# Self-attention over four images in split-operand products: the next image's projection moved into the steps of the present image's attention

## The chip, the cores and the metric

The kernel runs on one core of a Trainium2 chip. The core has a matrix engine (PE, with its weight loads shown apart as PEld), a vector engine (DVE), a scalar engine (ACT), a general engine (POOL) and a queue processor (SP). Each executes its own instructions strictly in the order in which the program wrote them and waits for the others by semaphores. POOL and SP issue the transfers between the on-chip memory (SBUF) and device memory (HBM). The metric is the device time of one execution in microseconds.

## The reference, cut to what matters

There are four images of 64 x 64 positions with 256 channels. Each is projected to q and k (128 channels each) and v (256 channels). The arrays are then reshaped, without a transposition, so that attention runs over 4096 columns; the softmax is over the 4096 columns of k.

```python
q = einsum('bwhc,cd->bwhd', x, Wq) + bq      # k with Wk, bk; v with Wv, bv
pq, pk, pv = (t.reshape(B, -1, N) for t in (q, k, v))   # N = 4096
attention = softmax(einsum('bcn,bcm->bnm', pq, pk), axis=-1)
out = einsum('bcm,bnm->bcn', pv, attention).reshape(x.shape)
return gamma * out + x
```

## The kernel before

**Split operands.** The matrix engine is used with operands of type fp32r, one pass for a product instead of fp32's two. To keep the precision, each fp32 operand y is written as three forms: h, a rounded and scaled upper part, l, what is left of y, and d, the slightly enlarged h less y. Three fp32r products of like forms (h by h, l by l, d by d) then stand for the one fp32 product. Each set of forms costs one ACT instruction (h) and two DVE instructions (l and d).

**Projection of an image.** 16 iterations i, each over 256 positions. `transposed` (L115) loads x through SP's queue, makes four PE transposes and one ACT copy. `qk` (L131) makes four fp32 products for q and k, and DVE adds the bias. `v` (L152) does the same for v, with the bias added by ACT. In `project_qk` (L254) ACT and DVE make the forms of q and k, and POOL writes them to HBM in three transfers: `kf` in one of contiguous runs of 3072 bytes a partition, `qd` in two of 1536 bytes. In `halve_v` (L275) the forms of v go to the resident tiles `vh`, `vl`, `vd`. All these products are fp32, two passes each.

**Attention of an image.** 128 steps u: 8 groups of 512 columns of q (index g) by 16 steps t, each with two blocks of 128 columns of k. In step u the code writes, in this order: `cross` for step u+3 (two products d by d, L308, each then scaled in place in PSUM by ACT, L309), the first half of `attend` for u (six products, L365), `energy` for u+2 (four products onto the same banks, L323, and two exponentials on ACT, L326), `upper` for u+2 (the form h of the exponentials, ACT, L332), `load_k` for u+5 (POOL, L296), `halves` for u+1 (DVE: running sum L341, form l L346, form d L348), and the second half of `attend` (six products). So PE has 18 products of 512 columns in a step.

**At a group's end.** `emptied` (L379) reads the four output banks a0, b0, a1, b1 with ACT, `sum_forms` and `sums` add the exponentials over the partitions (two products L396), and the generator `finish` is continued by one piece a step: reciprocal by way of HBM, normalisation on DVE (L410, L418), an accumulating load of x (POOL, L422) and the store (SP, L425).

**Buffers.** The eight PSUM banks are four for energies (`ps_e`) and four for outputs (`ps_o`); the projection borrows from both. Four buffers hold k tiles (`kpool`), three the exponentials x, two the forms `ld`, which the forms of q and k use too. POOL issues a k load as soon as the buffer is free and all POOL instructions written before it are issued.

**Order of images.** Image 0 is projected, then attended; then the projection of image 1 runs (only its first loads and transposes start in the last steps before), and so on. During a projection there is next to no attention work.

Of the kernel before, what the change touches and what calls it, by code (L numbers as in the profile page):

```python
# [9 lines left out]
F32 = mybir.dt.float32  # L10
# [10 lines left out]
def kernel(  # L21
# [54 lines left out]
    xv, ov = columns(x, XB), columns(out, XB)  # L76

    const = ctx.enter_context(tc.tile_pool(name="const", bufs=1))

    def load_x(pool, b, g):  # L80
        t = pool.tile([P, 2, XB], F32, tag="x", name=f"x_{b}_{g}")
        nc.sync.dma_start(t, xv[b, g])
        return t
# [6 lines left out]
    wqk_sb = const.tile([P, KC, 2 * C2], F32, name="wqk_sb")  # L90
    bqk_sb = const.tile([P, 2 * C2], F32, name="bqk_sb")
    nc.gpsimd.dma_start(bqk_sb[:, :C2], bq.partition_broadcast(P))
    nc.gpsimd.dma_start(bqk_sb[:, C2:], bk.partition_broadcast(P))
    wv_sb = const.tile([P, KC, C], F32, name="wv_sb")
    nc.gpsimd.dma_start(wv_sb, wv.rearrange("(k p) e -> p k e", p=P))
    bv_sb = const.tile([P, KC], F32, name="bv_sb")
    for eh in range(KC):
        nc.gpsimd.dma_start(bv_sb[:, eh : eh + 1], bv[eh * P : (eh + 1) * P].unsqueeze(1))
    gam2 = const.tile([P, 2], F32, name="gam")
    gam, gam1 = gam2[:, :1], gam2[:, 1:]  # L100
    nc.gpsimd.dma_start(gam, gamma.partition_broadcast(P))

    class Projection:


        def __init__(self, b, xpool, psum, xt_out, qk_out, v_out):
            self.b, self.xpool, self.psum = b, xpool, psum
            self.xt_out, self.qk_out, self.v_out = xt_out, qk_out, v_out
            self.xs, self.xt = {}, {}

        def load(self, g):
            if g < NI and g not in self.xs:
                self.xs[g] = load_x(self.xpool, self.b, g)

        def transposed(self, i):  # L115

            for g in range(i, i + 2):
                self.load(g)
            pool, tag = self.psum()
            tp = pool.tile([P, KC, 2, P], F32, tag=tag, name=f"xt_{self.b}_{i}")  # L120
            for k in range(KC):
                for s in range(2):
                    nc.tensor.transpose(
                        tp[:, k, s, :],
                        self.xs[i][:, s, k * P : (k + 1) * P],
                        ident,
                    )
            self.xt[i] = self.xt_out(i)
            nc.scalar.copy(self.xt[i], tp)  # L129

        def qk(self, i):  # L131
            pool, tag = self.psum()
            qk = pool.tile([P, 2, 2 * C2], F32, tag=tag, name=f"qk_{self.b}_{i}")
            for s in range(2):
                for k in range(KC):
                    nc.tensor.matmul(  # L136
                        qk[:, s, :],
                        self.xt[i][:, k, s, :],
                        wqk_sb[:, k, :],
                        start=(k == 0),  # L140
                        stop=(k == KC - 1),
                    )
            for dst, o in self.qk_out(i):
                w = dst.shape[2]
                nc.vector.tensor_tensor(  # L145
                    dst,
                    qk[:, :, o : o + w],
                    bqk_sb[:, o : o + w].unsqueeze(1).to_broadcast([P, 2, w]),
                    ALU.add,
                )  # L150

        def v(self, i):  # L152
            pool, tag = self.psum()
            vp = pool.tile([P, KC, C], F32, tag=tag, name=f"v_{self.b}_{i}")
            for eh in range(KC):
                for k in range(KC):
                    nc.tensor.matmul(  # L157
                        vp[:, eh, :],
                        wv_sb[:, k, eh * P : (eh + 1) * P],
                        self.xt[i][:, k].rearrange("p s a -> p (s a)"),  # L160
                        start=(k == 0),
                        stop=(k == KC - 1),
                    )
            to, bias, scale = self.v_out(i)
            for eh in range(KC):
                nc.scalar.activation(  # L166
                    to[:, eh, :],
                    vp[:, eh, :],
                    AF.Identity,
                    bias=bias[:, eh : eh + 1],  # L170
                    scale=scale,
                )
# [7 lines left out]
    E = 2.0**-12  # L180


    UPPER = 1.0 - 2.0**-13

    xg, og = columns(x, NB), columns(out, NB)
    again = const.tile([P, 1], I32, name="again")
    zs = const.tile([P, 1], F32, name="zs")
    rall = const.tile([P, B * NG, NJ], F32, name="rall")
    bv4_sb = const.tile([P, KC], F32, name="bv4_sb")
    nc.gpsimd.tensor_scalar(bv4_sb, bv_sb, 1.0 / E, None, ALU.mult)  # L190
    nc.gpsimd.tensor_scalar(gam1, gam, 1.0 + E, None, ALU.mult)

# [6 lines left out]
    with ExitStack() as fast:  # L199
# [4 lines left out]
        xpool, xtpool, qkv = pool("xpool", 3), pool("xtpool", 3), pool("qkv", 1)  # L204
        ppool = pool("ppool", 2)
        work = pool("work", 2)
        kpool = pool("kpool", 4)
        dram = pool("dram", 2, space=DRAM)
        ps_e = pool("ps_e", 4, space=PSUM)
# [3 lines left out]
        vh, vl, vd = (  # L213
            qkv.tile([P, NM, C], F32R, tag=name, name=name) for name in ("vh", "vl", "vd")
        )
        zd, rd = (dram.tile([B * NG, NB], F32, tag=n, name=n, bufs=1) for n in ("zd", "rd"))
        nc.scalar.dma_start(wqk_sb[:, :, :C2], wq.rearrange("(k p) d -> p k d", p=P))
        nc.scalar.dma_start(wqk_sb[:, :, C2:], wk.rearrange("(k p) d -> p k d", p=P))

        images, qd, kf, units, loads, now = [], {}, {}, {}, {}, {}  # L220

        energies = cycle([(ps_e, "e")])
        outputs = cycle([(ps_o, "a0"), (ps_o, "a1"), (ps_o, "b0"), (ps_o, "b1")])
        active = []

        def start(pieces):
            active.append(pieces)
            next(pieces)
# [5 lines left out]

        def image(b):
            def xt_out(i):
                return xtpool.tile([P, KC, 2, P], F32, tag="xt", name=f"xts_{b}_{i}")

            def qk_out(i):
                now["qk"] = work.tile([P, 2, 2, C2], F32, tag="qk", name=f"qks_{b}_{i}")  # L240
                return tuple((now["qk"][:, w], w * C2) for w in range(2))

            def v_out(i):
                now["v4"] = work.tile([P, KC, C], F32, tag="v4", name=f"v4_{b}_{i}")
                return now["v4"], bv4_sb, 1.0 / E

            images.append(Projection(b, xpool, lambda: next(now["banks"]), xt_out, qk_out, v_out))

            for g in range(NG):
                qd[b, g] = dram.tile([P, NJ, 3, P], F32R, tag=f"qd{g}", name=f"qd_{b}_{g}")  # L250
            for t in range(NU):
                kf[b, t] = dram.tile([P, 2, 3, P], F32R, tag=f"kf{t}", name=f"kf_{b}_{t}")

        def project_qk(b, i):  # L254
            images[b].qk(i)
            qk = now["qk"]
# [8 lines left out]
            for s in range(2):  # L265
                nc.gpsimd.dma_start(qd[b, i // NJ + NG // 2 * s][:, i % NJ], f[:, 0, s])
# [430 lines left out]
```

## Time and profile before

The three runs shown took 2433.49, 2436.36 (median) and 2436.83 us.

| what | value |
|---|---|
| time of the profiled execution | 2433.35 us |
| its span | 2431.6 us, granted PE clock 0.997 |
| busy share PE / PEld / DVE / ACT / POOL | 98% / 81% / 85% / 76% / 18% |
| 512-column fp32r products (18 x 512 steps) | 9216 |
| period of a group of 16 steps | 66.47 us |
| moved through the DMA queues | 338.22 MB, mean 139 GB/s |

PE's busy share counts a product from its issue to its modelled end, and neighbours overlap; so what a product costs is read from the distance between starts, not from its duration. In the groups of instructions the number after x is how many there are, then come total busy time, mean duration, and the idle time before them with what ended it. A line of the timeline has start, length, engine, line of the code, operation and tiles; several like instructions in a row are merged, and then the length runs from the first start to the last end. A group's period is read from any instruction that occurs once a group.

### The profile page before, as it was taken

What the parts mean: (1) busy time and instruction counts of PE and PEld (TensorE: products, weight loads), DVE (VectorE), ACT (ScalarE), POOL (GpSimd) and SP (SyncE); (2) the same over time, 40 slices, a digit from 0 to 9 for tenths busy, and PEclk for the clock granted to TensorE, in tenths of its full rate; (3) what the DMA queues carried; (4) which work ended last, traced back from release to release, by engine and by line L of the source; (5) the groups of instructions that cost most, each with busy time, mean ns of one, the idle gap of its engine ahead of it and who ended that gap; (6) DMA issues with size and microseconds to landing.
All of it is one profiled execution on the core that took longest, in us unless ns stands there. A gap on an engine that the chain in (4) does not pass through costs nothing.

```text
span 2431.6 us, 30522 instructions
## 1 busy us (share of the span) xinstructions
PE 2385.8 (98%) x10588; PEld 1963.4 (81%) x10588; DVE 2071.1 (85%) x2058; ACT 1851.9 (76%) x3071; POOL 429.2 (18%) x781
## 2 busy tenths in 40 slices
PE   9999999999999999999999999999999999999998
PEld 7788888888778888888887888888888788888886
DVE  5888888888698888888879888888887988888887
ACT  5778778777578878778767778787776777878775
POOL 4211111111321111111032111111113111111110
PEclk9999999999999999999999999999999999999999
DMA  8544444454854444444485544444448544444443
GB/s 257 155 123 123 127 120 122 132 133 104 248 164 128 116 129 116 128 130 127 107 263 155 129 130 117 126 118 126 130 105 266 150 128 132 125 118 129 114 124 90
DMA packets 155215, 338.22 MB, mean 139 GB/s; under 512 B 23471, under 2 KB 56751, under 8 KB 155054
## 3 DMA queue, kind: packets, MB, share of 16 engines
q0 software_dynamic: 114656, 293.52, 44.8%
q1 hardware_dynamic: 39854, 42.41, 6.0%
q8 instruction: 87, 1.43, 0.2%
q14 instruction: 74, 0.61, 0.1%
q10 hardware_dynamic: 544, 0.26, 0.0%
HBM read 268.89 MB, written 67.24 MB: 138 GB/s over the span
## 4 chain that ended last, share of the span: by engine, by line
PE 80%; ACT 11%; DMA 4%; DVE 2%; issue 2%; POOL 0%; ACTq 0%; DVEq 0%; POOLq 0%
PE a L365 34%; PE e L323 17%; PE b L365 17%; PE e L308 8%; DMA qd<-f 4%; ACT o L379 3%; ACT h L332 2%; ACT s L326 1%; PE qk L136 1%; ACT x L326 1%; PE z L396 1%; PE v L157 1%; ACT v L166 1%; ACT f L259 1%; ACT e L309 1%
## 5 line engine op out<-in xcount | busy, mean ns | idle before, releaser
L326 ACT ACTIVATE x<-e 128x512 f32<-128x512 f32 x960 | 520.8, 595 | 402.2 <-PE e L323 402.2
L341 DVE TENSOR_TENSOR s<-s,x 128x1024 f32<-128x1024 f32 x480 | 587.4, 1224 | 167.7 <-ACT x L326 159.0
L365 PE MATMUL b<-ld,vd 128*128 128x512 f32 x2048 | 632.1, 390 | 4.3 <-DVE ld L348 4.1
L365 PE MATMUL a<-ld,vl 128*128 128x512 f32 x2048 | 631.1, 389 | 4.8 <-DVE ld L346 4.8
L365 PE MATMUL a<-h,vh 128*128 128x512 f32 x2048 | 631.7, 390 | 0.5 <-ACT v L166 0.5
L346 DVE TENSOR_TENSOR ld<-x,h 128x1024 fp32r<-128x1024 f32 x480 | 584.5, 1218 | 3.7 <-DMA qd<-f 3.7
L348 DVE SCALAR_TENSOR_TENSOR ld<-h,x 128x1024 fp32r<-128x1024 f32 x480 | 584.6, 1218 | 0.0
L296 POOL DMA_DIRECT2D k<-kf x512 | 273.7, 535 | 1680.0 <-PE e L323 1546.9
L323 PE MATMUL e<-q,k 128*128 128x512 f32 x2048 | 548.7, 390 | 0.7 <-ACT e L309 0.7
L309 ACT ACTIVATE e<-e 128x512 f32<-128x512 f32 x1024 | 544.8, 566 | 0.0
L332 ACT ACTIVATE h<-x 128x1024 fp32r<-128x1024 f32 x480 | 509.9, 1062 | 14.9
L365 PEld LDWEIGHTS b<-ld,vd 128*128 128x128 f32 x2048 | 383.2, 188 | 89.0 <-DVE ld L348 7.5
L365 PEld LDWEIGHTS a<-ld,vl 128*128 128x128 f32 x2048 | 384.0, 188 | 86.6 <-DVE ld L346 6.5
L323 PEld LDWEIGHTS e<-q,k 128*128 128x128 f32 x2048 | 383.6, 188 | 81.4 <-ACT e L309 1.6
L365 PEld LDWEIGHTS a<-h,vh 128*128 128x128 f32 x2048 | 384.1, 188 | 80.1 <-ACT v L166 1.0
L308 PE MATMUL e<-q,k 128*128 128x512 f32 x1024 | 318.6, 392 | 0.0
L308 PEld LDWEIGHTS e<-q,k 128*128 128x128 f32 x1024 | 191.9, 188 | 44.5 <-ACT x L326 6.1
L261 DVE SCALAR_TENSOR_TENSOR f<-f,qks 128x512 fp32r<-128x512 f32 x128 | 82.8, 688 | 67.8 <-ACT f L259 67.8
L136 PE MATMUL qk<-wqk_sb,xts 128*128 128x256 f32 x512 | 125.3, 388 | 2.1 <-ACT xts L129 1.9
L157 PE MATMUL v<-xts,wv_sb 128*128 128x256 f32 x512 | 120.8, 380 | 0.0
L259 ACT ACTIVATE f<-qks 128x512 fp32r<-128x512 f32 x64 | 40.4, 631 | 100.9 <-DVE qks L145 58.5
L136 PEld LDWEIGHTS qk<-wqk_sb,xts 128*128 128x128 f32 x512 | 95.0, 193 | 17.7 <-ACT xts L129 5.2
(68 smaller groups left out, 1040.2 us busy)
## 6 DMA issues: line engine op xcount, KB each, us to landing
k<-kf POOLq DMA_DIRECT2D x512, 384.0 KB, 3.4
kf<-f POOLq DMA_DIRECT2D x64, 384.0 KB, 3.1
qd<-f POOLq DMA_DIRECT2D x128, 192.0 KB, 3.8
q<-qd POOLq DMA_DIRECT2D x32, 768.0 KB, 5.1
x<-in_x_dram SPq DMA_DIRECT2D x64, 256.0 KB
o<-in_x_dram POOLq DMA_DIRECT2D x31, 512.0 KB, 5.9
out_dram<-o SPq DMA_DIRECT2D x31, 512.0 KB
r<-rd SPq DMA_DIRECT2D x31, 256.0 KB
```

The lines of the kernel that those rows point to most:

```text
L136: nc.tensor.matmul(qk[:, s, :], self.xt[i][:, k, s, :], wqk_sb[:, k, :], start=(k == 0), stop=(k == KC - 1),)
L157: nc.tensor.matmul(vp[:, eh, :], wv_sb[:, k, eh * P : (eh + 1) * P], self.xt[i][:, k].rearrange("p s a -> p (s a)"), start=(k == 0), stop= ...
L296: nc.gpsimd.dma_start(t, kf[b, u % NU])
L308: nc.tensor.matmul(e, *forms(b, u, i, 2), start=True, stop=False, skip_group_check=True)
L309: nc.scalar.mul(e, e, -1.0 / (1.0 + E))
L323: nc.tensor.matmul(e, *forms(b, u, i, f), start=False, stop=(f == 1), skip_group_check=True)
L326: nc.scalar.activation(x[:, i, :], e, AF.Exp, scale=(1.0 + E) / E)
L332: nc.scalar.activation(h, units[b, u], AF.Identity, scale=UPPER)
L341: nc.vector.tensor_tensor(s, s, x, ALU.add)
L346: nc.vector.tensor_tensor(l, x, h.bitcast(F32), ALU.subtract)
L348: nc.vector.scalar_tensor_tensor(d, h.bitcast(F32), 1.0 + E, x, ALU.mult, ALU.subtract)
L365: nc.tensor.matmul(to, (vh, vl, vd)[f][:, t + NU * i, j * P : (j + 1) * P], units[b, u][f][:, i, :], start=(t == 0 and i == 0 and f != 1), ...
```

## The change

The projection of image b+1 no longer stands between two attentions. It is cut into 16 iterations of eight steps each, and runs inside the 128 steps of image b's attention. The function `step` is called three times in each step, for the PE, the ACT and the DVE part; r is the step's number in its eight.

- The projection's products become fp32r: x gets forms h, l, d (`x_forms`), the weights get theirs once at the start (`weights`, into `wf`), and `products` makes 12 products of 256 columns for q and k and 12 for v in place of four fp32 products each. The d-by-d products come first; `seed_qk` (DVE) and `seed_v` (ACT) scale that partial sum in PSUM and add the bias; the other eight accumulate on top.
- PE: transposes at r = 0, d-by-d products at r = 3 and 5, the others at r = 4 and 6. ACT: one form at r = 1, 5 and 7, two seeds at r = 6. DVE: one instruction of 128 x 512 in each step but r = 4.
- The forms of q and k of an iteration lie in another order, with q and k side by side in each form. POOL writes them at r = 6 in four transfers, each of three runs of 512 bytes a partition.
- The forms of v of images 1 to 3 are written to HBM (`vf`, 6144 bytes a partition) at the next r = 0, and read back into the one resident tile `vall`, one sixteenth a step from three steps after the last group's start (`load_v`, POOL).
- `cross` is now for step n+2, in the same step as its `energy`. `load_k` is for n+4 and stands after the step's POOL writes. The energies have two PSUM banks instead of four, the projection two of its own, k tiles have three buffers instead of four, the exponentials two instead of three. The second `emptied` of a group and `sums` move to the next group's first step. `finish` has its pieces spaced differently.
- Image 0 is projected ahead of its attention, in the same split products; its v forms go straight to `vall`. The attention's steps are numbered through all images.

```diff
--- before.py
+++ after.py
...
-        xpool, xtpool, qkv = pool("xpool", 3), pool("xtpool", 3), pool("qkv", 1)
+        qkv = pool("qkv", 1)
         ppool = pool("ppool", 2)
         work = pool("work", 2)
-        kpool = pool("kpool", 4)
+        kpool = pool("kpool", 3)
         dram = pool("dram", 2, space=DRAM)
-        ps_e = pool("ps_e", 4, space=PSUM)
+        ps_e = pool("ps_e", 2, space=PSUM)
+        ps_p = pool("ps_p", 2, space=PSUM)
         ps_o = pool("ps_o", 1, space=PSUM)
-        vh, vl, vd = (
-            qkv.tile([P, NM, C], F32R, tag=name, name=name) for name in ("vh", "vl", "vd")
-        )
+        vall = qkv.tile([P, NU, 3, 2, C], F32R, tag="v", name="v")
+        wf = qkv.tile([P, 2, 3, KC, C], F32R, tag="wf", name="wf")
...
+        def split(h, l, d, y, scale=E):
+
+            nc.scalar.activation(h, y, AF.Identity, scale=UPPER * scale)
+            yield
+            for t, f in ((l, 1.0 / scale), (d, 1.0 / scale + 1.0)):
+                nc.vector.scalar_tensor_tensor(t, h.bitcast(F32), -f, y, ALU.mult, ALU.add)
+                yield
...
+        def load_x(b, i):
...
+        def x_forms(b, i):
...
+            h = f[:, 0]
+            nc.scalar.activation(h, y, AF.Identity, scale=UPPER)
+            yield
+            nc.vector.tensor_tensor(f[:, 1], y, h.bitcast(F32), ALU.subtract)
+            yield
+            nc.vector.scalar_tensor_tensor(f[:, 2], h.bitcast(F32), 1.0 + E, y, ALU.mult, ALU.subtract)
+            yield
+
+        def products(b, i, w, fs):
+
+            xf = units["xf", b, i]
+            if fs[0] == 2:
+                units[w, b, i] = bank(f"qv{w}_{b}_{i}", [P, 2, C])
+            to = units[w, b, i]
+            for f in fs:
+                for s in range(2):
+                    for k in range(KC):
+                        if w:
+                            left, right = wf[:, 1, f, k, s * P : (s + 1) * P], xf[:, f, k]
+                        else:
+                            left, right = xf[:, f, k, s, :], wf[:, 0, f, k]
+                        nc.tensor.matmul(
+                            to[:, s, :],
+                            left,
+                            right.rearrange("p s a -> p (s a)") if w else right,
+                            start=(f == 2 and s == k == 0),
+                            stop=(f == 1 and k == KC - 1),
+                            skip_group_check=True,
+                        )
+
+        def seed_qk(b, i):
+            y = units[0, b, i]
+            nc.vector.scalar_tensor_tensor(
+                y, y, REST, bias.unsqueeze(1).to_broadcast([P, 2, C]), ALU.mult, ALU.add
+            )
+
+        def seed_v(b, i):
+            y = units[1, b, i]
+            for eh in range(KC):
+                nc.scalar.activation(
+                    y[:, eh, :], y[:, eh, :], AF.Identity, bias=bvs[:, eh : eh + 1], scale=REST
+                )
+
+        def qk_forms(b, i):
+            y = units.pop((0, b, i))
+            f = work.tile([P, 2, 3, C], F32R, tag="pf", name=f"f_{b}_{i}")
+            h = f[:, :, 0, :]
+            nc.scalar.activation(h, y, AF.Identity, scale=UPPER / 64)
+            yield
...
+                nc.vector.scalar_tensor_tensor(f[:, :, j, :], h.bitcast(F32), s, y, ALU.mult, op)
+                yield
-            nc.gpsimd.dma_start(kf[b, i], f[:, 1])
             for s in range(2):
+                nc.gpsimd.dma_start(kf[b, i // 2 + NU // 2 * s][:, i % 2], f[:, s, :, C2:])
+                nc.gpsimd.dma_start(qd[b, i // NJ + NG // 2 * s][:, i % NJ], f[:, s, :, :C2])
...
+        def v_forms(b, i):
+            y = units.pop((1, b, i))
+            units.pop(("xf", b, i))
+            if b == 0:
+                f = vall[:, i]
+            else:
+                f = work.tile([P, 3, 2, C], F32R, tag="pf", name=f"vf_{b}_{i}")
+            yield from split(f[:, 0], f[:, 1], f[:, 2], y)
+            if b:
+                nc.gpsimd.dma_start(vf[b, i], f)
+
+        def load_v(b, t):
+            nc.gpsimd.dma_start(vall[:, t], vf[b, t])
...
+        def load_k(n):
+            b, u = divmod(n, STEPS)
+            if b < B:
                 t = kpool.tile([P, 2, 3, P], F32R, tag="k", name=f"k_{b}_{u}")
                 nc.gpsimd.dma_start(t, kf[b, u % NU])
...
+        def step(n, engine):
+
+            b, u = divmod(n, STEPS)
+            i, r = divmod(u, R)
+            b += 1
+            made = now["made"]
+            if engine == "pe" and b < B:
+                if r == 0:
+                    transposed(b, i)
+                elif r == 3:
+                    products(b, i, 0, (2,))
+                elif r == 4:
+                    products(b, i, 0, (0, 1))
+                elif r == 5:
+                    products(b, i, 1, (2,))
+                elif r == 6:
+                    products(b, i, 1, (0, 1))
+            elif engine == "act" and b < B:
+                if r == 1:
+                    made["x"] = x_forms(b, i)
+                    next(made["x"])
+                    load_x(b, i + 1)
+                elif r == 5:
+                    made["qk"] = qk_forms(b, i)
+                    next(made["qk"])
+                elif r == 6:
+                    seed_v(b, i)
+                elif r == 7:
+                    made["v"] = v_forms(b, i)
+                    next(made["v"])
+            elif engine == "dve":
+                if r == 0 and "v" in made:
+                    for _ in made.pop("v"):
+                        pass
+                if b < B:
+                    if r in (1, 2):
+                        next(made["x"])
+                    elif r == 3:
+                        seed_qk(b, i)
+                    elif r == 5:
+                        next(made["qk"])
+                    elif r == 6:
+                        for _ in made.pop("qk"):
+                            pass
+                    elif r == 7:
+                        next(made["v"])
...
+        for i in range(NI):
+            load_x(0, i + 3)
+            if i + 1 < NI:
+                transposed(0, i + 1)
+                xs = x_forms(0, i + 1)
+            else:
+                xs = iter(())
+            products(0, i, 0, (2,))
+            seed_qk(0, i)
+            products(0, i, 1, (2,))
+            next(xs, None)
+            seed_v(0, i)
+            if i in (12, 14):
+                cross(i // 2 - 6)
+            products(0, i, 0, (0, 1))
+            qk = qk_forms(0, i)
+            next(qk)
+            products(0, i, 1, (0, 1))
+            if i in (12, 14):
+                energy(i // 2 - 6)
+            vs = v_forms(0, i)
+            next(vs)
+            for _ in xs:
+                pass
+            for _ in qk:
+                pass
+            for _ in vs:
+                pass
+            if i in (13, 15):
+                upper(i // 2 - 6)
             if i == 6:
...
+                load_q(0, 0)
+            if i in (6, 7, 8, 13):
+                load_k(i - 6 if i < 13 else 3)
+        halves(0)
+        now["banks"] = cycle([(ps_p, "p")])
+        for n in range(B * STEPS):
+            b, u = divmod(n, STEPS)
+            g, t = divmod(u, NU)
+            final = n == B * STEPS - 1
+            if u == 0 and b + 1 < B:
+                image(b + 1)
+                load_x(b + 1, 0)
+            if n == B * STEPS - 6:
+                xr = ppool.tile([P, 2, NB], F32, tag="s", name="xr")
...
+            cross(n + LOOK)
+            if t == 0 and n:
+                emptied(n - 1, 1)
+            if t == NU - 1 and not final:
+                sum_forms(n)
+            step(n, "act")
+            if not final:
+                attend(n, 0)
+            energy(n + LOOK)
+            if t == 0 and n:
+                sums(n - 1)
+                active.append(finish(n // NU - 1, now["o"], now["total"]))
+            if t == NU - 1 and not final:
+                emptied(n, 0)
+            upper(n + LOOK)
+            step(n, "pe")
+            halves(n + 1)
+            step(n, "dve")
+            if final:
+                finish_last(n, xr)
+                break
+            attend(n, 1)
+            load_k(n + LOOK + 2)
+            if t == 6 and n + NU < B * STEPS:
+                load_q(*divmod(n // NU + 1, NG))
+            if n >= STEPS - NU + 3 and (n - 3) // NU % NG == NG - 1 and (n - 3) // STEPS + 1 < B:
+                load_v((n - 3) // STEPS + 1, (n - 3) % NU)
+            proceed()
```

The helpers not shown (`transposed`, `load_x`, `weights`, `image`, `bank`) hold what the text above says of them, and the class `Projection` is kept for the fallback at the kernel's end, which the runs don't enter.

## The prediction

> **What bounds the kernel now.** I read the page first, for shares and rows:
>
> ```profile
> span 2431.6 us, 30522 instructions
> PE 80%; ACT 11%; DMA 4%; DVE 2%; issue 2%; POOL 0%; ACTq 0%; DVEq 0%; POOLq 0%
> L296 POOL DMA_DIRECT2D k<-kf x512 | 273.7, 535 | 1680.0 <-PE e L323 1546.9
> L261 DVE SCALAR_TENSOR_TENSOR f<-f,qks 128x512 fp32r<-128x512 f32 x128 | 82.8, 688 | 67.8 <-ACT f L259 67.8
> ```
>
> PE carries the chain of waits, and POOL waits 3.4 us for each k load (1546.9 over 450): k is early today. Then busy time by stage: image 0's projection, its attention, image 1's projection.
>
> ```profile
> 7.00:78.00 71.00, 68.56 (x340) 58.34 (x338) 49.25 (x92) 44.54 (x90) 27.46 (x53) 1.00 0.86 259
> 78.00:608.00 530.00, 524.95 (x2305) 430.83 (x2305) 465.42 (x418) 417.10 (x679) 78.33 (x140) 1.00 0.47 123
> 608.00:684.00 76.00, 70.91 (x340) 59.66 (x338) 51.52 (x94) 47.39 (x94) 28.62 (x55) 0.98 0.79 237
> ```
>
> The third column before the end is the PE clock, the last two are DMA share and GB/s: projection is where the DMA engines are busy. Then one step in the timeline, to time the change step by step:
>
> ```profile
> 300.10 0.61 PE L308 MATMUL e<-q,k 128*128 128x512 f32 x2
> 300.57 1.06 ACT L309 ACTIVATE e<-e 128x512 f32<-128x512 f32 x2
> 301.88 1.22 DVE L348 SCALAR_TENSOR_TENSOR ld<-h,x 128x1024 fp32r<-128x1024 f32 x1
> 301.91 1.07 PE L323 MATMUL e<-q,k 128*128 128x512 f32 x4
> 302.56 1.09 ACT L326 ACTIVATE x<-e 128x512 f32<-128x512 f32 x2 [0.93 <-PE e L323]
> 303.28 0.53 POOL L296 DMA_DIRECT2D k<-kf  x1 [3.02 <-PE e L323]
> 303.68 1.06 ACT L332 ACTIVATE h<-x 128x1024 fp32r<-128x1024 f32 x1
> 304.18 0.61 PE L308 MATMUL e<-q,k 128*128 128x512 f32 x2
> ```
>
> A step is 304.18 - 300.10 = 4.08 us, 18 products at 0.2267, PE without a gap. ACT has 0.93 free, DVE 0.58.
>
> **Removed: three projections.** The last `emptied` of images 0, 1, 2 stands at 607.90, 1212.70, 1814.77 in the chain of waits; less eight groups of 66.47 the two distances leave 73.0 and 70.3. With their mean for the third: -214.9.
>
> **Added on PE: 48 iterations of four transposes and 24 products of 256 columns.** No such fp32r product is in the trace. The rows nearest:
>
> ```profile
> 2419.59 0.30 PEld L457 LDWEIGHTS rp<-last,ones 128*128 128x128 f32 x2 [0.86 <-DVE last L445]
> 662.87 0.60 PE L123 MATMUL xt<-ident,x 128*128 128x128 f32 x4
> 663.30 1.89 PE L136 MATMUL qk<-wqk_sb,xts 128*128 128x256 f32 x8
> ```
>
> An instruction alone lasts 276 ns (L123) and 388 (L136), so starts stand (600 - 276)/3 = 108 and (1890 - 388)/7 = 215 ns apart. The 107 ns between them are 128 columns at the two-pass pace, so 256 at the fp32r pace; 512 cost 227. One product of 256 thus costs from 113 (half) to 227 - 107 = 120; I take 117. The weight load is the doubt: it lasts 188 ns, and if it can't hide, a product costs 188 + 4 = 192, the upper end. I take it as hidden, since two loads in a row (first line) last 0.30 together, so follow each other by 0.11. One iteration is 4 x 0.108 + 24 x 0.117 = 3.24; 48 make +155.7.
>
> A rule speaks against this. The Trainium skill, "TensorE: Matmul & The Clock Gate", Part 3 (packing small matmuls), says that a weight load overlaps matmuls in flight only for another row group; every load here takes all rows. By it a product is an estimated 107 + 109 = 216 ns and the sum 114 us more. The trace disagrees: a 188 ns load and 512 columns fit into 227.
>
> **Image 0's projection** is bound by DVE: seven instructions of 0.62 (L261's 0.688, starts 0.6 to 0.65 apart) and a wait of 0.7 for the q and k form, 5.0 an iteration where PE needs 3.24. The narrow writes (below) add 4.05 us of transfer to x's 0.93, 4.98, so a DMA share near 1; I take 5.4. 16 make 86; ahead of them stand the weights' four ACT and four DVE instructions (first product at 10 instead of 8.5), behind them the last forms and two early energies, some 7. Step 1 begins near 104 instead of 83.92: +20. Bounds: +3 (DVE's 4.35 alone) to +37 (POOL at 6.6, below).
>
> **Inside a step** r of the eight, from its first product: cross to 0.45, attend to 1.81, energies to 2.72, projection, attend. ACT scales until 1.5, then its projection instruction (0.6; two of 0.41 at r = 6) fits into the free 0.93 before the exponentials at 2.46: nothing; without that cover 0.6 us in each of four steps of eight. Two energy banks suffice, as the exponentials end at 3.5, before the next cross at 4.08. DVE needs 3.42 + 0.62 = 4.04 against PE's mean of 4.08 + 3.24/8 = 4.49: nothing, though without the gap it would cost up to 0.6 a step. x loads (SP, 7 steps ahead), reads of `vf` (13 steps ahead) and the respaced `finish` hide behind those distances; the reads bring the last group's transfers to some 4.4 us a step, just under its length.
>
> **Group's end.** `emptied` now delays the scaling (PE 0.46) and the products of `sums` wait for its second half (0.7): 1.16 instead of 0.6 seen before L396. +0.56 a group; in image 3's eight groups +4.
>
> **The k load behind four narrow writes** decides. At r = 6 POOL issues the q and k writes, then k for n+4. It can't overtake, and the step's first product two steps on waits for it. DVE ends the last form at 3.2 (l at 0.2, d 1.35, form 2.5); at t = 14 the half-sum (L352, 0.68) makes it 3.85. The write's POOL time is not in the trace with 384 runs: 128 runs take 0.53; the weight load L95 with 256 took 0.736 next to 0.56, the accumulating load L422 with 256 took 1.095. So 0.53 to 1.65, and I take 0.87 from L95, the only plain one. Four take 3.5, and k is issued at 6.7. It lands 3.4 later:
>
> ```profile
> DMA to landing us min/median/max: 3.0/3.4/9.2
> ```
>
> at 10.1. The transfer says later: single packets in the trace took 80 ns for 1536 bytes, 136 for 3072 and 249 for 6144, a line that gives 42 for 512; 1536 of them on 16 engines last 4.05, and k's own 1.09 and its fixed part of 2.3 come behind, 10.7. I take 10.4. Needed it is at 5.02 (r = 6) + 4.08 (r = 7) = 9.1. Late by 1.3 and, at t = 14, by 1.95; the second covers the group's 0.6. Net 2.65 a group, 24 groups: +64. Bounds: +13 (in time, only the 0.56 left) to +198 (POOL 1.65: late 4.1 and 4.75).
>
> At r = 0 the v form's write (0.53 on POOL, 2.0 of transfer at 249 ns for 6144 bytes) goes ahead of k in the same way: DVE ends it at 3.75, k is issued at 4.3 and lands between 7.7 and 9.0; needed at 4.08 + 0.44 + 4.08 = 8.6. I take nothing; at most 0.4 a group, 10 in all.
>
> **Sum.** 2431.6 - 214.9 + 155.7 + 20 + 4 + 64 = 2460.4 span. The profiled execution took 1.75 more than its span and was 3.0 below the median; so in terms of the median I forecast 2465, 1.2% slower.
>
> **Rivals.**
> - *Faster: k is in time.* Place: POOL's queue at r = 6. Price: 64 becomes 13, so 2414. It decides if the four writes and k's landing fit into the 5.9 us between 3.2 and 9.1, that is if k is issued by 5.7. For: POOL's rows are flat at 0.53 from 1536 to 6144 bytes a run; if they are flat in the number of runs too, k is issued at 5.3; and landings go down to 3.0. Against: the transfer of 4.05. The Trainium skill, "DMA: Bandwidth & Descriptors", Anatomy of one DMA, calls descriptor generation small, many descriptors coming before it shows; by that this case holds, but L95 (0.736 to 0.56) leans the other way.
> - *Weight loads bind the 256-column products* (192 ns): +24 x 48 x 0.075 = +86, so 2549. The skill's rule above would put it higher still. For: 188 ns exceed 107. Against: the 0.30 for two loads.
> - *POOL pays by L422's row:* +134 on the k load and +17 ahead, 2614. Against: L422 also accumulates.
>
> **Chances.** Forecast 0.52 (2435 to 2490), k in time 0.33 (2398 to 2430), weight loads 0.09, POOL 0.06. What a measurement of this kernel tells from no change is about 0.2%, 4.9 us. The seam of the first two, 2431 to 2441, holds 0.04. So faster 0.32, same 0.04, slower 0.64. The range reaches from inside the faster case to short of the weight-load one: 2402 to 2535, which leaves out 0.04 below and 0.13 above.
>
> **What would show it.** The distance between starts of the 256-column products (0.117 against 0.192). A PE gap at the first product of steps with r = 0, released by the k load: 1 to 2 us twice a group in images 0 to 2, none in image 3. POOL's duration for `kf` and `qd` writes (0.87 against 0.53 or 1.65). The start of step 1 near 104. A group's period near 75.6 in images 0 to 2 (73.5 if k is in time), 67 in image 3. Wrong I am if the gap is missing, or if DVE or ACT rather than k is what PE waits for within a step.

## The result, and the profile after

The changed kernel took 2588.49 us (median of four runs, 2586.50 to 2592.37), the kernel before beside it 2435.41: a ratio of 1.0631, 95% interval 1.0613 to 1.0649. It is 6.3% slower, 153 us, where 1.2% was forecast and the range ended at 2535. The profiled execution took 2586.5 us.

The page of the changed kernel: span, busy shares, the costliest rows, and the landing times of two queues.

```profile
span 2584.7 us, 31929 instructions
PE 2392.0 (93%) x11096; PEld 1968.0 (76%) x11096; DVE 2150.5 (83%) x2126; ACT 1881.7 (73%) x3075; POOL 582.3 (23%) x942
L286 POOL DMA_DIRECT2D k<-kf x512 | 284.9, 557 | 1153.6 <-PE e L314 934.7
L299 PE MATMUL e<-q,k 128*128 128x512 f32 x1024 | 325.6, 399 | 140.3 <-DMA k<-kf 138.2
L260 POOL DMA_DIRECT2D kf<-f x128 | 98.4, 769 | 518.1 <-ACT x L317 221.1
k<-kf POOLq DMA_DIRECT2D x512, 384.0 KB, 4.1
vf<-vf POOLq DMA_DIRECT2D x48, 768.0 KB, 4.5
```

PE was 98% busy and is now 93%. The row of the cross products (L299) says why: 138.2 us of idle PE end with a k load. The rows of POOL give the price that was unknown: a narrow write is 769 ns, a k load 557. By stage (image 0's projection, then the attention of images 0, 2 and 3; image 1's is like image 2's; the columns as in the table before the change):

```profile
7.00:109.70 102.70, 71.58 (x496) 65.21 (x497) 78.52 (x123) 51.69 (x98) 54.69 (x73) 0.97 0.89 190
109.70:745.00 635.30, 591.38 (x2745) 486.50 (x2743) 529.28 (x522) 466.74 (x761) 144.87 (x233) 0.99 0.59 162
1390.00:2036.00 646.00, 596.35 (x2768) 489.19 (x2768) 537.66 (x530) 471.46 (x768) 149.17 (x240) 0.99 0.62 170
2036.00:2574.00 538.00, 533.04 (x2318) 434.84 (x2319) 464.97 (x421) 418.49 (x679) 80.53 (x143) 1.00 0.49 131
```

In the last stage, where nothing of a next image is left, PE is 99% busy and the DMA share 0.49; an attention before the change had 0.47. In the stages with a projection inside, PE stands idle for 44 to 50 us an image although the DMA engines are busy for only 0.6 of the time. One stretch of image 0's attention shows both places. First POOL (two issues between 377.67 and 384.76, a load of q and the next step's k load, are left out):

```profile
374.58 0.76 POOL L260 DMA_DIRECT2D kf<-f  x1 [9.71 <-ACT x L317]
375.34 0.79 POOL L261 DMA_DIRECT2D qd<-f  x1
376.12 0.78 POOL L260 DMA_DIRECT2D kf<-f  x1
376.89 0.78 POOL L261 DMA_DIRECT2D qd<-f  x1
377.67 0.59 POOL L286 DMA_DIRECT2D k<-kf  x1
384.76 0.54 POOL L272 DMA_DIRECT2D vf<-vf  x1 [5.43 <-issue]
385.29 0.54 POOL L286 DMA_DIRECT2D k<-kf  x1
385.81 1.15 POOL L411 DMA_DIRECT2D o<-in_x_dram  x1
```

and PE's lines of the two products that wait, each behind the last product of the step before:

```profile
379.49 0.61 PE L356 MATMUL b<-ld,v 128*128 128x512 f32 x2
381.91 0.70 PE L299 MATMUL e<-q,k 128*128 128x512 f32 x2 [1.80 <-DMA k<-kf]
390.21 0.61 PE L356 MATMUL b<-ld,v 128*128 128x512 f32 x2
392.42 0.70 PE L299 MATMUL e<-q,k 128*128 128x512 f32 x2 [1.59 <-DMA k<-kf]
```

The first wait (r = 0) is the one that was forecast: four writes at r = 6, k issued behind them at 377.67. The second (r = 2) was costed at nothing: the v form's write at 384.76 goes ahead of the k load at 385.29, and that load is in place only when PE starts at 392.42. So two late k loads stand in each eight steps, four in a group. In images 0 to 2, from the second group on, the mean length of a step (the distance between the cross products of neighbouring steps) is 6.11 us at r = 7 (it holds the wait at the next r = 0), 5.20 at r = 1, and 4.08 for a plain step.

### The profile page after: what moved, and what is told of

Its sections match the earlier page's. It is cut to its first block, busy times and chain, and to the rows that moved or that the text cites. A ratio compares the mean times of both kernels' runs of the same rounds, so it can differ in the third digit from the quotient of the medians.

```text
span 2584.7 us, 31929 instructions
## 1 busy us (share of the span) xinstructions
PE 2392.0 (93%) x11096; PEld 1968.0 (76%) x11096; DVE 2150.5 (83%) x2126; ACT 1881.7 (73%) x3075; POOL 582.3 (23%) x942
## 5 line engine op out<-in xcount | busy, mean ns | idle before, releaser
L356 PE MATMUL a<-h,v 128*128 128x512 f32 x2048 | 643.4, 395 | 0.0
L356 PE MATMUL a<-ld,v 128*128 128x512 f32 x2048 | 639.0, 393 | 2.4 <-DVE ld L337 2.4
L356 PE MATMUL b<-ld,v 128*128 128x512 f32 x2048 | 638.8, 393 | 0.1
L299 PE MATMUL e<-q,k 128*128 128x512 f32 x1024 | 325.6, 399 | 140.3 <-DMA k<-kf 138.2
L356 PEld LDWEIGHTS a<-ld,v 128*128 128x128 f32 x2048 | 387.3, 189 | 87.6 <-DVE ld L337 2.9
L356 PEld LDWEIGHTS b<-ld,v 128*128 128x128 f32 x2048 | 387.9, 190 | 85.1 <-ACT s L386 1.4
L356 PEld LDWEIGHTS a<-h,v 128*128 128x128 f32 x2048 | 370.8, 190 | 63.7 <-issue 0.6
L299 PEld LDWEIGHTS e<-q,k 128*128 128x128 f32 x1024 | 186.0, 189 | 208.5 <-issue 97.3
L228 PE MATMUL qv<-wf,xf 128*128 128x256 f32 x768 | 115.9, 287 | 24.0 <-DVE qv L239 22.5
L228 PEld LDWEIGHTS qv<-wf,xf 128*128 128x128 f32 x768 | 107.4, 191 | 35.5 <-DVE qv L239 25.6
L228 PEld LDWEIGHTS qv<-xf,wf 128*128 128x128 f32 x768 | 107.7, 192 | 7.5
L228 PE MATMUL qv<-xf,wf 128*128 128x256 f32 x768 | 112.8, 283 | 0.0
```

The lines of the kernel that those rows point to most:

```text
L228: nc.tensor.matmul(to[:, s, :], left, right.rearrange("p s a -> p (s a)") if w else right, start=(f == 2 and s == k == 0), stop=(f == 1 an ...
L299: nc.tensor.matmul(e, *forms(n, i, 2), start=True, stop=False, skip_group_check=True)
L356: nc.tensor.matmul(to, vall[:, t, f, i, j * P : (j + 1) * P], units[n][f][:, i, :], start=(t == 0 and i == 0 and f != 1), stop=(t == NU - ...
```

## The experiments

The kernel before took 2433.63, 2434.49 and 2434.59 us (medians) beside the three groups of experiments below.

### Which write makes which wait

Three kernels issue a k load ahead of the step's writes: in every step (`k_first`), only at r = 6, ahead of the q and k writes (`k_first_qk`), only at r = 0, ahead of the v write (`k_first_v`). In all other steps of the last two it keeps its place.

```diff
+            if not final:                   # k_first; k_first_qk: if n % R == 6
+                load_k(n + LOOK + 2)        # k_first_v: if n % R == 0
             step(n, "dve")
...
             attend(n, 1)
-            load_k(n + LOOK + 2)
```

> Edit: in every step the k load for n+4 stands ahead of the step's POOL writes instead of behind them; nothing else. In the changed kernel a group takes 80.3 us in images 0 to 2 where PE's own work is 66.95 + 2 x 3.31 = 73.6. Theory A (order in POOL's queue: k is issued only after the writes): the waits of the cross products for k (138 us, 83 times) vanish, and with them the 18 windows of half PE clock; a group takes 73.6 to 74.5, the kernel 2588 - 24 x 6.3 = 2435, between 2420 and 2450. Theory B (the DMA engines are too full for k in these steps whatever the order): k is issued earlier but still lands late; a group stays above 78, the kernel above 2540.

> Edit: the k load goes ahead of the four narrow q and k writes (r = 6) only; behind the write of the v forms (r = 0) it stays. Theory A: of some 6.7 us a group the two late loads of r = 6 carry 1.8 + 2.2 and most of the half-clock windows, so 2588 - 24 x 4.5 = 2480. As I predicted it (the v write costs at most 0.4 a group) it would be 2440 or less, the whole loss but 10 us. Theory B: above 2560.

> Edit: the k load goes ahead of the v write (r = 0) only; behind the narrow q and k writes it stays. Theory A: 2588 - 24 x 2.2 = 2535, the rest of what the load ahead of all writes gives, so that the two parts add up to it within 15 us. As I predicted it: 2578 or more. Theory B: above 2570.

| k load ahead of | median us | ratio to before (95%) | PE waits for k | step length at r = 7 / 0 / 1 / 2 |
|---|---|---|---|---|
| nothing (the change) | 2588.49 | 1.0631 (1.0613 to 1.0649) | 138.2 us, 83 times | 6.11 / 5.41 / 5.20 / 4.28 |
| the q and k writes | 2584.35 | 1.0617 (1.0596 to 1.0638) | 112.2 us, 55 times | 4.08 / 5.52 / 6.46 / 4.87 |
| the v write | 2536.6 | 1.0421 (1.0393 to 1.0449) | 93.0 us, 52 times | 6.00 / 5.39 / 4.10 / 4.29 |
| both | 2463.45 | 1.0118 (1.0101 to 1.0135) | 25.2 us, 25 times | 4.08 / 5.48 / 4.11 / 4.64 |

Step lengths are means over images 0 to 2 from the second group on.

Each move takes away exactly its own wait, so the order in POOL's queue is the cause of both: r = 7 falls to 4.08 with the first, r = 1 to 4.10 with the second. But the times don't add. Against the kernel with k ahead of both, the q and k writes in front of the load cost 73 us, the v write in front of it costs 121, and both together 125. The two waits stand in for each other. In `k_first_qk` the v write is issued 4.81 us after its step's first product (388.08 against 383.27), in the changed kernel 2.85 after (384.76 against 381.91): the v form doesn't move along with PE's wait, so when the wait at r = 0 goes, the write and the k load behind it stand that much later in the step, and what the step at r = 1 takes above a plain one grows from 1.1 to 2.4. The expectation for `k_first_qk` (2480) missed that; the one for `k_first_v` (2535) was met.

`k_first` stayed 28 us above its expectation. Its waits for k, in the view of waits:

```profile
PE e L299 <- DMA k<-kf: 25.2, 25, 4.0
```

stand for the most part in one place: 17 of the 25, 18 of the 25 us, are at t = 11, for the k load written at t = 9. On POOL it comes behind the v write of t = 8 and behind the accumulating load of x (L411) that follows it, and takes 7.6 us on average to land. The long landing is not the v write's doing: in `k_first_sp` below, where the v write has left POOL's queue and L411 has not, the same load still takes 7.0 us. But there it is issued 1.3 us before its step's first product, here 1.5 after, because POOL stands at the v write until the v form is done.

### Is it the transfers' shape, or the queue?

One kernel lays the forms of q and k out so that each write has one run of 1536 bytes a partition in place of three of 512. One leaves the order of the program as it is and issues the writes from SP's queue. One does that and has k ahead too.

```diff
-            f = work.tile([P, 2, 3, C], F32R, tag="pf", name=f"f_{b}_{i}")      # runs_1536
+            f = work.tile([P, 2, 2, 3, C2], F32R, tag="pf", name=f"f_{b}_{i}")
...
-            nc.gpsimd.dma_start(vf[b, i], f)                                    # sp_writes; kf, qd alike
+            nc.sync.dma_start(vf[b, i].bitcast(F32), f.bitcast(F32))
```

> Edit: the forms of q and k lie so that each of the four writes has one run of 1536 bytes a partition instead of three of 512; order and bytes as in the changed kernel. POOL's time for a write falls from 0.77 to 0.53 us (four: 1.0 less) and their transfer from about 4.0 to 2.4. k is issued 1.0 earlier and lands 1.0 to 2.0 earlier, so the late loads of r = 6 (1.8 and 2.2 us) shrink to about 0.6 and 1.0, and those of r = 0 stay: 2588 - 24 x 2.6 = 2525. If only the order counts and not the size of the runs: above 2570.

> Edit: the writes of the q, k and v forms are issued by SP instead of POOL; the k loads keep their place in the code, so nothing stands before them in POOL's queue but other loads and the accumulating x load. Theory A, order in POOL's queue: as with the k load moved ahead of all writes, 2463, between 2445 and 2480. Rival, shared transfer: the writes still move 192 KB and 768 KB through the same 16 DMA engines beside the k loads and k stays late: above 2540. A third outcome, a gain of about half (2490 to 2530), would say that issue order and transfer each carry a part.

> Edit: k load ahead of the step's writes, and the writes issued by SP. What is left in the k-first kernel is a wait of 0.6 to 1.6 us at t = 10, where the k load issued one step after the v write lands 7.3 us after its issue behind that write (4.3) and the accumulating load (7.1). If POOL's order is behind that too, the writes on SP end it: a group falls from 74.7 to 73.6, the kernel from 2463 to 2435. If it is the transfer, a group stays at 74.5 and more, the kernel at 2458 to 2475.

`runs_1536` took 2619.51 us (1.0762, 1.0740 to 1.0783), slower than the change. POOL's write did fall, from 769 to 536 ns, and the wait at r = 0 with it (5.34 at r = 7 instead of 6.11); but r = 1 went from 5.20 to 6.21 and r = 2 from 4.28 to 4.95, as in `k_first_qk`. PE's waits for k fall from 89.9 to 50.4 us at r = 0 and rise from 44.5 to 92.5 at r = 2, and the time at half the PE clock (below) rises from 61 to 96 us. The expected 2525 missed the second wait again.

`sp_writes` took 2431.79 us (0.9990, 0.9976 to 1.0005), level with the kernel before and better than either case expected. The same bytes in the same pieces move over the same DMA engines, and the waits for k are gone. Two of its lines of waits, and its page's line of the k loads:

```profile
PE e L303 <- DMA k<-kf: 1.0, 2, 0.7
PE xt L197 <- DMA x<-in_x_dram: 7.4, 2, 4.0
```

```profile
k<-kf POOLq DMA_DIRECT2D x512, 384.0 KB, 3.3
```

What has changed is when k is issued. The loads written at r = 6 and r = 0 now go out 0.9 to 1.4 us before the first product of their step (means); in the changed kernel it was 6.9 to 7.6 us after it at r = 6 and 3.5 to 4.5 after it at r = 0. The landing is not free of the writes. Most k loads of `sp_writes` meet none: 152 that met no write and none of POOL's other loads took 3.4 us on average, while the 16 that had at least half of a v form's write beside them took 5.3. Issued so early, they have that time. So what made k late is its place behind the writes in POOL's program, where POOL first stands until the forms are done; the added traffic costs about 2 us of landing where the two meet; and the shape of the writes, by `runs_1536`, is no cure while that place stays. The second line of waits is the same trap on SP: at the start of images 1 and 2 the load of x, which the changed kernel issued more than 25 us ahead, stands behind the last q and k writes, and PE waits for it once each.

With k ahead as well (`k_first_sp`) it is 2426.21 us (0.9975, 0.9959 to 0.9992), below the 2435 that was expected if POOL's order was behind the rest; PE's waits for k are 1.3 us there, where `k_first` had 25.2.

### What the gaps do to PE's clock

The changed kernel's trace has 18 windows of 3.4 us at half the PE clock, 61 us in all besides the end; the kernel before has a granted clock of 0.997, this one 0.986. Sixteen of them begin within 1.5 us of the end of a PE gap of 1.8 to 3.4 us that a k load ended; the other two are in image 0's projection. Not every gap has its window: there are 31 of 1.8 us or more. One of the sixteen, on PE:

```profile
298.61 0.61 PE L356 MATMUL b<-ld,v 128*128 128x512 f32 x2
301.23 0.70 PE L299 MATMUL e<-q,k 128*128 128x512 f32 x2 [2.00 <-DMA k<-kf]
301.77 0.65 PE L356 MATMUL a<-h,v 128*128 128x512 f32 x2
302.23 1.05 PE L356 MATMUL a<-ld,v 128*128 128x512 f32 x2
303.07 1.05 PE L356 MATMUL b<-ld,v 128*128 128x512 f32 x2
303.93 1.88 PE L314 MATMUL e<-q,k 128*128 128x512 f32 x4
```

After the gap of 2.00 us the four energy products need 1.88 us where they took 1.07 before the change. To tell what this costs, `fill` puts eight products without a use, 47 x 1.81 = 85 us of PE work, into the place of the wait at r = 0.

```diff
+            if n and n % R == 0 and b + 1 < B:
+                fill(b + 1, (n % STEPS) // R)   # 8 x matmul(tp, wf[...], wf[...], start=True, stop=True)
             cross(n + LOOK)
```

> Edit: the changed kernel with eight products of 512 columns on data at hand put before the cross products of each step with r = 0 but the first; their result is overwritten by the transposes that follow. They are 8 x 0.2267 = 1.8 us of extra PE work in the place where PE waits 1.9 to 2.2 us for k. If the half-clock windows (18 of 3.4 us each, so up to 18 x 1.7 = 30 us) come from these gaps and cost what they seem to, the windows fall below 6 and the kernel gains 15 to 30 us in spite of 85 us more PE work: 2558 to 2575. If the windows do not matter the time stays at 2585 to 2600; if the waits were not there, 2588 + 47 x 1.8 = 2673.

It took 2579.46 us (1.0599, 1.0578 to 1.0620), a little above the 2558 to 2575 expected. On PE:

```profile
379.04 0.61 PE L366 MATMUL b<-ld,v 128*128 128x512 f32 x2
379.49 1.98 PE L204 MATMUL xt<-wf 128*128 128x512 f32 x8
381.30 0.62 PE L309 MATMUL e<-q,k 128*128 128x512 f32 x2
```

Here the cross products start without a wait. The waits for k fall from 138.2 to 68.0 us, the half-clock windows from 18 to 4, and the kernel is 9 us faster although PE does 85 us more. So the gap was idle time that nothing else used. The 14 windows that are gone last 48 us, half of which is lost work, 24 us; 85 of added work, less 70 of waits, less 24, gives the 9 us. The waits at r = 0 go from 89.9 to 7.5 us, so the filling itself gains nothing, and those at r = 2 grow from 44.5 to 55.5: some of what the clock gives back goes into the next wait for k. That a slow step shortens that wait fits this but was not shown by itself.

### Does it beat the kernel before?

`k_first_v_later` has k ahead, writes the v form at r = 1 behind that step's k load, issues the accumulating load of x two steps later, and sets the tile of ones without waiting for the weights. `z_later` also moves `sums` and the start of `finish` from t = 0 to t = 1, into one of the projection's banks. `z_later_1536` also has the runs of 1536 bytes.

```diff
-                nc.gpsimd.dma_start(vf[b, i], f)                # k_first_v_later
+                now["vw"] = b, i, f
...
+            if n % R == 1 and "vw" in now:                      # behind load_k(n + LOOK + 2)
+                bb, ii, ff = now.pop("vw")
+                nc.gpsimd.dma_start(vf[bb, ii], ff)
...
-    nc.vector.tensor_scalar(ones_r, ident, 0.0, 1.0, ALU.mult, ALU.add)
+    nc.vector.memset(ones, 1.0)
...
-            if t == 0 and n:                                    # z_later
-                sums(n - 1)
+            if t == 1 and n > 1:
+                sums(n - 2)
```

> Edit: k load ahead of the step's writes; the v write issued one step later (r = 1, behind that step's k load); the accumulating load of x two steps later; the tile of ones set by a memset, so that the first PE work does not wait behind the weights' forms on DVE (PE's first product at 11.5 us now, 0.5 to 3 then). Theory: the k wait at t = 10 (1.1 us a group with its clock windows) goes, 24 x 1.1 + 17 us of half clock x 0.5 = -30, and the start saves 5 to 8: 2463 - 36 = 2427, between 2420 and 2440, that is faster than the kernel before by up to 0.5%. Rival: the wait only moves to the step after, as when the load was put ahead of the q and k writes alone: 2450 to 2465.

> Edit on the kernel with the later v write: the two products that add the exponentials over the partitions (sums) and the start of finish move from a group's first step to its second, and their bank is one of the projection's two instead of b1. At t = 0 a step lasts 6.18 us where PE's work is 4.97; I put 0.7 of the 1.2 down to these products waiting for the second emptied to free b1, the rest to the scaling behind ACT. Theory: t = 0 and t = 1 together get 0.6 to 0.7 shorter, 31 times: 2428 - 20 = 2408, between 2402 and 2414. Rival (ACT's queue sets that step's end, whatever waits on PE): the time stays within 2422 to 2430.

> Edit on the same: the q and k forms in runs of 1536 bytes, as in the runs-1536 kernel. With k ahead of the writes nothing waits for them: the writes are 1.0 us shorter on POOL and 1.6 in transfer, which nobody needs, so within 0.2% of the other kernel of this call; image 0's iterations, bound by DVE, stay at 5.0 us. Had the size of the runs a price of its own, as against the place in the queue, it would be 5 us or more faster.

| kernel | median us | ratio to before (95%) | commonest period of a group, images 0 to 2 / 3 |
|---|---|---|---|
| k_first_v_later | 2428.28 | 0.9976 (0.9966 to 0.9985) | 73.79 / 66.95 |
| z_later | 2417.59 | 0.9928 (0.9914 to 0.9941) | 73.17 / 66.41 |
| z_later_1536 | 2407.93 | 0.9890 (0.9875 to 0.9905) | 73.17 / 66.40 |

The first hit its expectation (2427); PE waits for k five times, 3.5 us in all. The second gained 11 us where 20 were expected. Its usual group is 0.62 shorter, as forecast, some 19 us in all; but in its profiled execution a few groups were longer, and PE's waits for k rose from 3.5 to 9.5 us, which is 6 of the 8 that are missing. The third gained 9.7 where nothing that could be told was expected, so once k no longer stands behind them, the longer runs do pay. Its usual group has the same period as the second's; of the 8.2 us between the two profiled spans (2414.9 and 2406.7) 6.2 are waits for k and 1.4 are in image 0's projection (step 1 at 104.7 us instead of 106.1). Whether POOL's shorter issue or the shorter transfers bring this was not separated. It is the fastest of all and 1.1% faster than the kernel before. From the views of waits of `z_later` and of `z_later_1536`, and the latter's page:

```profile
PE e L299 <- DMA k<-kf: 9.5, 6, 4.0
PE e L300 <- DMA k<-kf: 3.3, 4, 1.7
```

```profile
L261 POOL DMA_DIRECT2D kf<-f x128 | 68.6, 536 | 298.1 <-DVE f L258 232.2
```

## Why the prediction was wrong, by its own steps

- **The 256-column products** (taken 0.117 us apart, bounds 0.113 and 0.120, rival 0.192). Right. Eight of them in a row:

```profile
292.65 1.12 PE L228 MATMUL qv<-xf,wf 128*128 128x256 f32 x8
```

  At 283 ns for one, starts are (1.12 - 0.283)/7 = 0.120 apart, the upper end of the two that were weighed. An iteration is 3.31, 48 are 158.9 instead of 155.7. The rival of weight loads that bind falls, and with it, for this kernel, the rule of the Trainium skill, "TensorE: Matmul & The Clock Gate", Part 3, by which the sum was 114 us more: every load here takes all rows and still hides.
- **Image 0's projection** (+20, step 1 near 104). It began at 109.70, +25.8. The iterations were 5.04 apart, better than the 5.4 taken; the start was worse. The first product came at 17.50 instead of 10:

```profile
17.50 0.74 PE L228 MATMUL qv<-wf,xf 128*128 128x256 f32 x4 [1.50 <-DVE xf L212]
```

  What held it is in the view of waits: `wp`, a warm-up product, waits 6.6 us for the tile of ones, which DVE made behind the weights' four forms. Made without them (`k_first_v_later`), the first product comes at 12.8 and step 1 at 106.3.
- **A group's end** (+0.56). Right where it can be seen alone: image 3's groups are 66.95 instead of 66.47. In images 0 to 2, the usual 73.79 with k in time leaves 73.79 - 66.47 - 2 x 3.31 = 0.70.
- **DVE and ACT inside the step** (nothing). Right: steps with r = 3 to 6 are 4.59, 5.06, 4.58 and 5.06 long, a plain step of 4.08 with its PE products and nothing else.
- **The k load at r = 6** (POOL 0.87 a write, k issued 6.7 after the step's start, landed at 10.4, late by 1.3 and, at t = 14, by 1.95). Right in mechanism, too small in size. A write takes POOL 0.77 to 0.78; at the place shown, a t = 6, k is issued at 377.67 - 370.81 = 6.86, and PE waits 1.80. Against the usual step lengths of `k_first_v_later`, where k is in time, the steps at r = 7 are 1.90 and 2.17 longer, and of that the group's end gives back 0.39 where 0.6 was forecast (means of the changed kernel from the second group on). With the group's end (0.70) this is 4.38 a group, 105 us in all, where the term had 64. The bounds from 128 runs (0.53) and from the accumulating load (1.65) are both refuted; POOL's time does grow with the number of runs, from 0.53 at 128 to 0.77 at 384, and the faster rival falls with that. The Trainium skill, "DMA: Bandwidth & Descriptors", Anatomy of one DMA, calls that growth small; four times 0.24 us here was half of the 1.80.
- **The failed step: the v form's write at r = 0**, of which the prediction said "I take nothing; at most 0.4 a group, 10 in all". Its order was seen, and the k load behind it was put in place between 7.7 and 9.0 after the step's start, with 8.6 needed. At the place shown (t = 8) it was issued sooner than forecast (3.38 instead of 4.3) and yet landed at 392.29, 7.0 us after its issue and 10.4 after the step's start. On average such loads land 10.1 (t = 0) and 10.0 (t = 8) after it, 5.7 and 6.6 after their issue, where the forecast had 3.4 to 4.7. The write itself was not dear: with 2.0 of transfer and the prediction's own fixed part of 2.3 it should take 4.3, and its median is 4.5 (the one shown 5.4). What was priced too low is the load behind it. The write's packets run from 385.87 to 389.70, k's from 387.99 to 391.89, and from 390.75 on the accumulating load of x (L411) has packets in flight as well. So k's first packet comes 2.7 us after its issue, where loads without such company start after about 1.2, and in this stretch packets of 6144 bytes have a mean of 291 ns and k's of 3072 bytes 238 (median 136), where lone ones had 249 and 136. By step lengths the steps at r = 1 and 2 are 2.6 us longer a group in all: 63 us over 24 groups where the prediction had nothing.
- **The sum.** The waits at r = 0 and r = 2 were to be added, 64 and nothing. Measured, a group of images 0 to 2 takes 80.5 us on average: 66.47 before, 6.62 for two iterations, 0.70 for the group's end, and 6.7 for the late k loads where the forecast had 2.1 beyond the 0.56. Over 24 groups this is 161 us, and -214.9 + 24 x (80.5 - 66.47) + 3.8 + 25.8 = 151, against a measured difference of spans of 153.1. The same sum for `sp_writes`, whose groups average 74.32 and whose step 1 begins at 108.40, gives +1.8, measured +1.8, so the account closes to within some 2 us in both. The span was missed by 124 us: some 63 for the second wait, 41 for the first with the group's end, 12 for the step at t = 8, which is 0.5 longer and comes right behind the first wait, 6 for image 0 and 3 for the products. So the second wait is half of it, and the mis-sized first one most of the rest. `k_first_v` keeps only the wait that was forecast, and its 2536.6 is still 72 above 2465. Nor can the two be added as the prediction did, since the second wait grows when the first goes (`k_first_qk`).
- **The rival "k is in time"** (2414, a span of 2409) was low by 24 against `sp_writes`: 3 for the products, 5 for image 0, 3 for the group's end, and 13 for a few longer groups (24 x (74.32 - 73.79)), most of them at the changes of image, which no step of the prediction had; PE's waits for the load of x are 7.4 of the 13.

The half clock after the gaps was not in the prediction at all. The 16 windows behind the gaps are 55 us at half the clock, 27 of lost work, which is enough to explain why the gaps cost a little more than their own length (138.2 waited, some 161 lost); how the rest divides between clock and other delays was not separated.

## What to carry to other kernels

A load that a steady loop waits for must not be written behind a transfer that waits for slower work on the same queue: look at every queue that the new writes go through, and put the load ahead, or the writes elsewhere. When two waits stand within a few steps of each other, don't add their prices or expect one repair to pay by its own row; the second wait grows when the first goes, and here the two repairs alone gained 4 and 52 us, both together 125. Price a transfer that has company by a row with company.

## What the runs showed of the hardware

- Transfers in flight together held each other up, on two queues as on one. In `sp_writes` a k load of 384 KB took 5.3 us to land beside a 768 KB write on SP's queue (mean of 16) and 3.4 without company (mean of 152); right behind such a write on POOL's queue, in the changed kernel, it took 5.7 and 6.6 (t = 0 and t = 8). What moving the writes to SP took away was the late issue.
- A DMA of POOL costs it time by its runs: 0.53 to 0.54 us with 128 runs of 1536 or 6144 bytes, 0.77 with 384 runs of 512 bytes.
- PE gaps of about 2 us were enough to bring a window of 3.4 us at half the clock, though not each time: 16 behind waits for k in the changed kernel, where 31 such gaps lasted 1.8 us or more, and 2 in `fill`. The Trainium skill, "TensorE: Matmul & The Clock Gate", Why this matters for your kernels, asks for no gaps above about 3 us; the gap of 2.00 ahead of 301.23 was shorter and had its window all the same.
- Products of 256 columns in fp32r run 0.120 us apart although each has a weight load of about 0.19.
